# A pairwise attention kernel: exponentials for three slots at a time, the background work in one long turn per three

## The chip, the cores and the metric

The kernel runs on one core of one Trainium2 chip. The metric is the device time of that core in microseconds, from one launch; the numbers quoted are medians over several runs.

## The reference

Eight images of 128 channels and 36 x 36 points pass through three stages. The first is a convolutional attention layer (group norm, 3 x 3 convolutions for keys, values and queries, a softmax attention, two 1 x 1 convolutions, a residual). The second takes each point as a token and computes additive attention within an image of 1296 tokens; it is where nearly all the time goes. The third is a small mixture of experts.

```
def _L1_attn_ref(x, mask, Wq, bq, Wk, bk, w, bw):
    q = jnp.einsum('bld,ed->ble', x, Wq) + bq
    k = jnp.einsum('bld,ed->ble', x, Wk) + bk
    t = jnp.tanh(q[:, :, None, :] + k[:, None, :, :])
    scores = jnp.einsum('bijd,d->bij', t, w) + bw[0]
    attn = jax.nn.softmax(scores, axis=-1)
    return jnp.einsum('bij,bjd->bid', attn, x)
```

The tanh stands between every query and every key, so there are 1296 x 1296 scores of 128 terms each for every image.

## The kernel before, in words

The tanh of a sum of a query's and a key's value is written as a quotient. Five or six feature channels are taken together: with products of exponentials over all sign patterns, a matrix product over 32 or 64 rows gives a common denominator d, and another, with weighted queries, the numerator n. The score is the sum of n/d over 24 such groups. The quotient is n * exp(-ln d).

**Units and slots.** A unit is one image b, one chunk c of 432 queries (three per image) and one tile j of keys: ten tiles of 128 keys and one remainder tile of 16, which stands sixth in the order (line 919). A full unit has 12 slots (lines 49 to 54), in the repeating order five, five, six: a slot with fives has two products over 32 rows each, a slot with sixes two over 64 rows each. The halves of the array that the fives use alternate, so the numerators of slot p and the denominators of slot p + 3 fit beside each other. Every product is a 432 column float32 matmul into one PSUM bank, and each is two matmul instructions in the profile. A remainder unit has two slots. In all there are 240 full units and 24 remainders, 2928 slots. I call three slots in sequence a three; a full unit has four.

**A slot's work** (lines 1113 to 1146). In iteration p: `take_turns` runs background steps that are not matmuls; `numerators(p)` issues two matmuls into two banks of the pool `ps_n` (tag n, four banks in all); `denominators(p + LAG)`, with LAG 3, issues the matmuls for three slots later into a buffer of two banks of `ps_d` (two such buffers, four banks in all), and on ScalarE the logarithm of both banks at once (line 972) into a tile lq; each odd slot also issues the exponential over the tile's two slots (line 975). Then `terms(p)` multiplies n by lq on VectorE. In eight of the 12 slots it writes the products to rp (line 1003), and GpSimd adds them up (lines 1010 and 1012). In the four of `DVE_PAIRS` VectorE does both itself: two multiplies in place in PSUM (line 997, in the unit's first such slot 992 and 993) and two additions (line 999, in the first 994); those banks come free with the last addition. At a unit's end GpSimd folds the two sums (lines 1019 and 1021), and seven slots later ScalarE takes the score's exponential (line 1032).

**The background.** Everything else (layer 0 of the next image, its tokens and key features, the query features, weighing the tokens with the finished scores, the gate) is written as generators in four lanes: `first_of_all` (query blocks and remainders), `urgent` (the attending), `gates` and `background` (line 1067). A generator yields ahead of a matmul step or of another step, with a number of slots to rest. A matmul step takes a bank of the same pool `ps_n` through `aux`, and a later step empties it, on VectorE or ScalarE. `matmul_turn` (line 1077) runs after each slot and issues at most one matmul step: matmuls are counted in columns in `behind`, and `balance` gets PACE columns per slot; lanes other than `first_of_all` wait when the balance is negative or the next slot is one of `DVE_PAIRS`. The step that empties the bank follows in `take_turns` of the next slot (TAKE has a rest of 1), and not in a slot of `DVE_PAIRS`. Key tiles are written to DRAM and come back through SyncE's queue two units ahead (`prefetch`).

Each engine runs its instructions in the order of the program text; a pool's buffers are handed out in turn, and a new use waits for the last reader of the old one.

Of the kernel before, what the change touches and what calls it, by code (L numbers as in the profile page):

```python
# [10 lines left out]
F32 = mybir.dt.float32  # L11
# [9 lines left out]
CH = 432  # L21
# [6 lines left out]
NKT = len(KT)  # L28
# [17 lines left out]
NF = 8  # L46
FIVES = 4 * 5 * (NF // 2)

SLOTS = []
# [6 lines left out]
IN_TURN = [m + i for m in range(NF // 2) for i in (0, NF // 2)]  # L56
LAG = 3
SHIFT = 6.5
DVE_PAIRS = (2, 5, 8, 11)
PACE = 400  # L60

# [7 lines left out]
def kernel(  # L71
# [58 lines left out]
    with ExitStack() as loop, ExitStack() as score:  # L130

        def pool(name, bufs, stack=loop, side="left", space=bass.MemoryType.SB):
            return stack.enter_context(
                tc.tile_pool(name=name, bufs=bufs, side=side, space=space)
            )
# [7 lines left out]
        kfp = pool("kfp", 3, score, "right")  # L143
        kstp = pool("kstp", 3, score, "right")
        qfp = pool("qfp", NF + 1, score, "right")
        lp = pool("lp", 3, score, "right")
        rpp = pool("rpp", 3, score, "right")
        acc = pool("acc", 2, score, "right")
        ps_d = pool("ps_d", 2, score, "right", bass.MemoryType.PSUM)
# [119 lines left out]

        TAKE = (False, 1)

        def step(rest=1):
            return (False, rest)
# [645 lines left out]
        slots = []  # L921
        for u, (b, c, j) in enumerate(units):
            slots += [(u, k) for k in range(len(REM_SLOTS) if j == NKT - 1 else NP)]
        kf_of, qf_of, lq_of, live = {}, {}, {}, {}

        def prefetch(u):
            if u < len(units) and u not in kf_of:
# [9 lines left out]
        def new_block(b, c, q):  # L937
            qf = qfp.tile([128, 2, CH], F32, tag="qf", name="qf")
            qf_of[b, c, q] = qf
            return query_block(b, c, q, qf)  # L940
# [13 lines left out]
                    mm(out[32 * i : 32 * i + 32, :CH], kf[rows, q, :32],  # L954
                       qf_of[b, c, q][rows, part, :], start=True, stop=True)

        def banks(u, k):
            return 2 if units[u][2] < NKT - 1 else len(REM_SLOTS[k])

        def denominators(p):  # L960

            if p >= len(slots):
                return
            u, k = slots[p]
            d = ps_d.tile([128, 2, 512], F32, tag="d", name="d")
            n = banks(u, k)
            products(u, k, 0, [d[:, h, :] for h in range(n)])
            if k % 2 == 0:
                lq_of[u, k // 2] = lp.tile([128, 4, CH], F32, tag="lq", name="lq")
            lq = lq_of[u, k // 2]  # L970
            o = 2 * (k % 2)
            nc.scalar.activation(lq[:, o : o + n, :], d[:, :n, :CH], AF.Ln)  # L972
            if k % 2 == 1:
                some = lq[:, : o + n, :]
                nc.scalar.activation(some, some, AF.Exp, scale=-1.0)  # L975

        def numerators(p):
            ns = [ps_n.tile([128, 512], F32, tag="n", name="n") for _ in range(banks(*slots[p]))]
            products(*slots[p], 1, ns)
            return [ps[:, :CH] for ps in ns]  # L980

        def terms(p, ns):

            u, k = slots[p]
            lq = lq_of[u, k // 2]
            o = 2 * (k % 2)
            mult = nc.vector.tensor_mul
            rem = units[u][2] == NKT - 1
            if k in DVE_PAIRS and not rem:
                if k == DVE_PAIRS[0]:  # L990
                    live["d"] = acc.tile([128, CH], F32, tag="accd", name="accd")
                    mult(live["d"], ns[0], lq[:, o, :])
                    mult(ns[1], ns[1], lq[:, o + 1, :])
                    nc.vector.tensor_add(live["d"], ns[1], live["d"])
                else:
                    for h in range(2):
                        mult(ns[h], ns[h], lq[:, o + h, :])  # L997
                    for h in range(2):
                        nc.vector.tensor_add(live["d"], ns[h], live["d"])  # L999
            else:  # L1000
                rp = rpp.tile([128, 2, CH], F32, tag="rp", name="rp")
                for h, n in enumerate(ns):
                    mult(rp[:, h, :], n, lq[:, o + h, :])  # L1003
                if rem:
                    live.setdefault("rem", []).extend(rp[:, h, :] for h in range(len(ns)))
                elif k == 0:
                    live["r"] = rp
                elif k == 1:
                    live["p"] = acc.tile([128, 2, CH], F32, tag="accp", name="accp")
                    nc.gpsimd.tensor_add(live["p"], live["r"], rp)  # L1010
                else:
                    nc.gpsimd.tensor_add(live["p"], live["p"], rp)  # L1012
            if k % 2 == 1:
                lq_of.pop((u, k // 2))

        def sums(u):

# [56 lines left out]
                if lane.due(p, False) and (k not in DVE_PAIRS or lane is first_of_all):  # L1074
                    lane.run(p)

        def matmul_turn(p, k):


            before = behind[0]  # L1080
            for lane in lanes:
                while lane.due(p, True) and behind[0] == before:
                    paced = balance[0] < 0 or k + 1 in DVE_PAIRS
                    if lane is not first_of_all and paced or lane is gates and urgent:
                        break
                    lane.run(p)
            balance[0] = min(balance[0] - (behind[0] - before) + PACE, 2 * PACE)

        drain(normal(0))
        for name in ("wv_t", "wq_t"):  # L1090
# [9 lines left out]
        a_q, a_k, cs_s, fb_s, eb_s = (feat[n] for n in ("a_q", "a_k", "cs_s", "fb_s", "eb_s"))  # L1100
        drain(tokens(0), keys(0, order[:1]))
        for i, q in enumerate(IN_TURN):
            if i < 3:
                drain(new_block(0, 0, q))
            else:
                first_of_all.append(new_block(0, 0, q))
# [6 lines left out]
        for p, (u, k) in enumerate(slots):  # L1113
            b, c, j = units[u]
            rem = j == NKT - 1
            if k == 0:
                prefetch(u + 2)
                if c == 0 and j == 1:
                    if b > 0:
                        gates.append(gating(b - 1))  # L1120
                    if b == NB - 1:
                        gates.append(residuals(4))
                    if b + 1 < NB:
                        background.extend(
                            (normal(b + 1), conv_keys(b + 1), layer0(b + 1), tokens(b + 1),
                             keys(b + 1, range(NKT)))
                        )
            take_turns(p, k)
            ns = numerators(p)
            denominators(p + LAG)  # L1130
            terms(p, ns)
            if pending and pending[0][0] <= p:
                exps(p, *pending.popleft()[1:])
            last = p + 1 == len(slots) or slots[p + 1][0] != u

            if j == order[-1] and u + 1 < len(units) and k % 3:
                used = IN_TURN.index(SLOTS[k][0]) + 1
                if used < NF:
                    first_of_all.append(new_block(*units[u + 1][:2], IN_TURN[used]))
            elif j == order[-2] and last and u + 2 < len(units):  # L1140
                first_of_all.append(new_block(*units[u + 2][:2], IN_TURN[0]))
            matmul_turn(p, k)
            if last and rem:
                first_of_all.append(rem_scores(p, u, live.pop("rem")))
            elif last:
                pending.append((p + 7, u, sums(u)))
# [211 lines left out]
```

The softmax here doesn't subtract the row's maximum and nothing guards it: scores larger than these inputs give would overflow.

## Time and profile before

| | |
|---|---|
| median of 3 runs | 6133.27 us (6131.81 to 6136.31) |
| the profiled execution: span | 6139.0 us, all of its own time |
| mean granted TensorE clock | 0.985 |
| ScalarE, Ln over 864 (line 972) | 2928 times, mean 878 ns |
| ScalarE, Exp over 1728 (line 975) | 1440 times, mean 1644 ns; 24 over 1296, 1284 ns |
| VectorE multiply to rp (line 1003) | 3912 times, mean 600 ns |
| VectorE's own multiplies and sums (lines 997, 999) | 1440 times each, mean 608 and 602 ns |
| GpSimd add over 864 (line 1012) | 1440 times, mean 2025 ns |

The slot loop runs from about 162 us to 5984 us of the span; what lies before is the first image's setup, what comes after is the experts. In the lines that follow, a group is given by its line, its engine and its operation, then the tile written and the tiles read, the shape and the count. In a timeline a line starts with the start and the duration in us, and a bracket at the end tells how long the engine was idle and what ended that. A wait is given as who waited, for whom, the sum in us, the number of waits and the longest. PE is TensorE, PEld its weight loads, DVE VectorE, ACT ScalarE, POOL GpSimd, SP SyncE.

### The profile page before, as it was taken

How to read it: one execution, taken by the hardware profiler on the slowest of the kernel's cores; microseconds unless marked ns; L12 is line 12 of the kernel's file. 1: busy time of each engine (PE TensorE's matmuls, PEld its weight loads, DVE VectorE, ACT ScalarE, POOL GpSimd, SP SyncE). 2: the span in 40 equal slices, each digit the busy share in tenths (PEclk: the TensorE clock that was granted, in tenths of full speed). 3: DMA queues.
4: the chain of work that ended last, by engine and by line, in shares of the span. 5: the costliest groups of instructions: out<-in, count | busy, mean ns of one | idle time of the engine just before them, and what ended most of it. 6: DMA issues, size and time to landing. Idle time of an engine off the chain costs nothing.

```text
span 6139.0 us, 93072 instructions
## 1 busy us (share of the span) xinstructions
PE 5957.9 (97%) x33480; PEld 2862.1 (47%) x33480; DVE 4796.4 (78%) x9521; ACT 5279.9 (86%) x5371; POOL 4597.7 (75%) x2819
## 2 busy tenths in 40 slices
PE   7999999999999999999999999999999999999996
PEld 5454444544544445444455444454444544544443
DVE  4787878877788787877888777887778877788882
ACT  1888898888988888889998889888898888999990
POOL 4777777777787777778778786877777777787870
PEclk9999999999999999999999999999999999999997
DMA  1210011100110002100111001110011100110008
GB/s 44 70 37 22 25 62 38 34 25 28 68 43 20 26 27 71 39 24 23 44 55 39 22 24 59 44 39 22 20 65 40 34 25 28 58 50 29 28 20 297
DMA packets 151519, 270.87 MB, mean 44 GB/s; under 512 B 45648, under 2 KB 76752, under 8 KB 151056
## 3 DMA queue, kind: packets, MB, share of 16 engines
q1 hardware_dynamic: 151056, 264.92, 13.0%
q8 instruction: 264, 4.33, 0.3%
q14 instruction: 199, 1.63, 0.1%
HBM read 200.41 MB, written 64.19 MB: 43 GB/s over the span
## 4 chain that ended last, share of the span: by engine, by line
PE 77%; ACT 7%; DVE 6%; issue 6%; POOL 2%; DMA 1%; SPq 0%; DVEq 0%; POOLq 0%; ACTq 0%
PE n L949 37%; PE d L949 12%; PE pa L284 7%; PE pc L284 5%; ACT lq L972 5%; PE s L284 3%; PE pk L284 3%; PE pq L284 3%; DVE rp L1003 2%; DVE n L997 1%; DVE accd L999 1%; PE d L954 1%; ACT lq L975 1%; DMA w<-in_weight_dram 1%; PE n L954 1%
## 5 line engine op out<-in xcount | busy, mean ns | idle before, releaser
L1012 POOL TENSOR_TENSOR accp<-accp,rp 128x864 f32<-128x864 f32 x1440 | 2915.8, 2025 | 1041.0 <-DVE rp L1003 948.8
L949 PE MATMUL n<-qf,kf 32*128 32x432 f32 (+1 forms) x11520 | 3325.3, 574 | 46.5 <-ACT e L1032 13.3
L949 PE MATMUL d<-qf,kf 32*128 32x432 f32 (+1 forms) x11520 | 2991.6, 561 | 38.7 <-ACT lq L972 38.2
L972 ACT ACTIVATE lq<-d 128x864 f32<-128x864 f32 x2928 | 2524.2, 878 | 542.6 <-PE d L949 512.1
L1003 DVE TENSOR_TENSOR rp<-n,lq 128x432 f32<-128x432 f32 x3912 | 2173.3, 600 | 743.5 <-PE d L949 542.8
L975 ACT ACTIVATE lq<-lq 128x1728 f32<-128x1728 f32 (+1 forms) x1464 | 2398.2, 1638 | 46.3
L949 PEld LDWEIGHTS n<-qf,kf 32*128 32x128 f32 (+1 forms) x11520 | 1206.4, 184 | 1600.3 <-DVE rp L1003 581.5
L949 PEld LDWEIGHTS d<-qf,kf 32*128 32x128 f32 (+1 forms) x11520 | 1090.0, 185 | 422.1 <-issue 224.7
L997 DVE TENSOR_TENSOR n<-n,lq 128x432 f32<-128x432 f32 x1440 | 814.9, 608 | 142.1 <-PE n L949 88.5
L999 DVE TENSOR_TENSOR accd<-n,accd 128x432 f32<-128x432 f32 x1440 | 866.3, 602 | 24.6
L1010 POOL TENSOR_TENSOR accp<-rp 128x864 f32<-128x864 f32 x240 | 485.2, 2022 | 197.7 <-DVE rp L1003 195.6
L711 POOL TENSOR_SCALAR qf<-qf,cs_s 128x432 f32<-128x432 f32 x192 | 260.9, 1365 | 45.0 <-ACT qf L710 44.4
L284 PEld LDWEIGHTS pa<-xh,e 128*108 128x108 f32 x1920 | 222.5, 174 | 131.1 <-DVE rp L1003 56.0
L1021 POOL TENSOR_TENSOR accd<-accp,accd 128x432 f32<-128x432 f32 x240 | 265.2, 1105 | 18.8
L1019 POOL TENSOR_TENSOR accp<-accp 128x432 f32<-128x432 f32 x240 | 264.4, 1102 | 16.7
L284 PE MATMUL pa<-xh,e 128*108 128x129 f32 x1920 | 262.9, 283 | 8.7 <-ACT e L1032 5.2
L284 PE MATMUL s<-q,k 128*116 128x432 f32 x480 | 230.3, 568 | 1.7 <-DVE q L316 1.4
L284 PEld LDWEIGHTS pk<-xT,a_k 128*128 128x128 f32 x1408 | 171.2, 192 | 107.0 <-DVE n L997 33.7
L462 POOL TENSOR_TENSOR tot<-tot,e 116x432 f32<-116x432 f32 x192 | 212.0, 1104 | 6.0 <-ACT e L471 4.6
L471 ACT ACTIVATE e<-s 116x432 f32<-116x432 f32 x240 | 124.9, 520 | 98.3 <-PE s L284 97.9
L284 PE MATMUL pa<-e,vw 116*128 116x432 f32 x480 | 204.6, 549 | 0.0
L284 PE MATMUL pk<-xT,a_k 128*128 128x128 f32 (+1 forms) x1408 | 202.5, 287 | 0.1
(213 smaller groups left out, 3788.4 us busy)
## 6 DMA issues: line engine op xcount, KB each, us to landing
kf<-kd SPq DMA_DIRECT2D x239, 512.0 KB
kd<-ks SPq DMA_DIRECT2D x158, 256.0 KB
w<-in_weight_dram SPq DMA_DIRECT2D x32, 1024.0 KB
wk_t<-wk_t_d SPq DMA_DIRECT2D x7, 768.0 KB
wv_t<-wv_t_d SPq DMA_DIRECT2D x7, 768.0 KB
wq_t<-wq_t_d SPq DMA_DIRECT2D x7, 768.0 KB
x<-in_x_dram SPq DMA_DIRECT2D x8, 648.0 KB
t<-tokd SPq DMA_DIRECT2D x96, 54.0 KB
```

The costliest lines, as they stand in the source:

```text
L284: mm(out, lhsT, rhs, **kw)
L711: nc.gpsimd.tensor_scalar(qf[:, 1, :], qf[:, 0, :], cs_s[:, q : q + 1], None, ALU.mult)
L949: mm(outs[h][:, :CH], kf[rows[h], q, :], qf_of[b, c, q][rows[h], part, :], start=True, stop=True)
L972: nc.scalar.activation(lq[:, o : o + n, :], d[:, :n, :CH], AF.Ln)
L975: nc.scalar.activation(some, some, AF.Exp, scale=-1.0)
L997: mult(ns[h], ns[h], lq[:, o + h, :])
L999: nc.vector.tensor_add(live["d"], ns[h], live["d"])
L1003: mult(rp[:, h, :], n, lq[:, o + h, :])
L1010: nc.gpsimd.tensor_add(live["p"], live["r"], rp)
L1012: nc.gpsimd.tensor_add(live["p"], live["p"], rp)
L1019: nc.gpsimd.tensor_add(s[:, 0, :], s[:, 0, :], s[:, 1, :])
L1021: nc.gpsimd.tensor_add(d, s[:, 0, :], d)
```

## The change

The parts, in order of the diff:

- VectorE's own sums move from the third slot of each three to the first, and the background gets its matmul turn only in that first slot (`TURNS`), with a credit of 380 columns per slot, up to 1520. A turn goes on until the credit is below zero or no lane has a matmul step due, and after each matmul step the steps that are due, such as emptying the bank, are issued at once (TAKE's rest is 0).
- The query blocks of the next unit follow a table (`NEXT_AT`), two after each of three slots; the last of them is made in the next chunk's first unit. One more is made ahead of the loop.
- Denominators come ahead of numerators in an iteration, except where the lq buffer is released by the same slot's multiplies (`late`).
- A tile lq holds six banks, for three slots; there are two of them instead of three of four banks. Groups end with the first slot of a three, or with the first of a remainder, so a group is the second and third slot of one three and the first of the next.
- GpSimd's first sum takes slots 1 and 2 instead of 0 and 1.

```diff
-DVE_PAIRS = (2, 5, 8, 11)
-PACE = 400
+DVE_PAIRS = (0, 3, 6, 9)
+TURNS = (0, 3, 6, 9)
+NEXT_AT = {3: IN_TURN[1:3], 6: IN_TURN[3:5], 9: IN_TURN[5:7]}
+PACE = 380
...
-        lp = pool("lp", 3, score, "right")
+        lp = pool("lp", 2, score, "right")
...
-        TAKE = (False, 1)
+        TAKE = (False, 0)
...
+        group_of, ends, at = {}, [-1], 0
+        for p, (u, k) in enumerate(slots):
+            group_of[p] = (len(ends), at)
+            at += banks(u, k)
+            rem = units[u][2] == NKT - 1
+            if p + 1 == len(slots) or (k == 0 if rem else k % 3 == 0):
+                assert at <= 6
+                ends.append(p)
+                at = 0
...
-            if k % 2 == 0:
-                lq_of[u, k // 2] = lp.tile([128, 4, CH], F32, tag="lq", name="lq")
-            lq = lq_of[u, k // 2]
-            o = 2 * (k % 2)
+            g, o = group_of[p]
+            if o == 0:
+                lq_of[g] = lp.tile([128, 6, CH], F32, tag="lq", name="lq")
+            lq = lq_of[g]
             nc.scalar.activation(lq[:, o : o + n, :], d[:, :n, :CH], AF.Ln)
-            if k % 2 == 1:
+            if p == ends[g]:
                 some = lq[:, : o + n, :]
                 nc.scalar.activation(some, some, AF.Exp, scale=-1.0)
...
-                elif k == 0:
+                elif k == 1:
                     live["r"] = rp
-                elif k == 1:
+                elif k == 2:
...
-        def matmul_turn(p, k):
-
-
-            before = behind[0]
-            for lane in lanes:
-                while lane.due(p, True) and behind[0] == before:
-                    paced = balance[0] < 0 or k + 1 in DVE_PAIRS
+        def matmul_turn(p, turn):
+
+
+            balance[0] = min(balance[0] + PACE, 4 * PACE)
+            while True:
+                for lane in lanes:
+                    paced = not turn or balance[0] < 0
                     if lane is not first_of_all and paced or lane is gates and urgent:
+                        continue
+                    if lane.due(p, True):
                         break
+                else:
+                    return
+                before = behind[0]
+                lane.run(p)
+                balance[0] -= behind[0] - before
+                while lane.due(p, False):
                     lane.run(p)
-            balance[0] = min(balance[0] - (behind[0] - before) + PACE, 2 * PACE)
...
-            if i < 3:
+            if i < 4:
...
-            ns = numerators(p)
-            denominators(p + LAG)
-            terms(p, ns)
+            ahead = p + LAG
+            g, o = group_of.get(ahead, (0, 1))
+            late = o == 0 and g > 2 and ends[g - 2] == p
+            if not late:
+                denominators(ahead)
+            terms(p, numerators(p))
+            if late:
+                denominators(ahead)
...
-            if j == order[-1] and u + 1 < len(units) and k % 3:
-                used = IN_TURN.index(SLOTS[k][0]) + 1
-                if used < NF:
-                    first_of_all.append(new_block(*units[u + 1][:2], IN_TURN[used]))
+            if j == order[-1] and u + 1 < len(units):
+                for q in NEXT_AT.get(k, ()):
+                    first_of_all.append(new_block(*units[u + 1][:2], q))
+            elif j == order[0] and k == TURNS[0] and u > 0:
+                first_of_all.append(new_block(b, c, IN_TURN[-1]))
...
-            matmul_turn(p, k)
+            matmul_turn(p, k == 1 if rem else k in TURNS)
```

More of the change, by code (lines that the diff above doesn't have):

```diff
@@ L923, with banks @@
             slots += [(u, k) for k in range(len(REM_SLOTS) if j == NKT - 1 else NP)]
+        def banks(u, k):
+            return 2 if units[u][2] < NKT - 1 else len(REM_SLOTS[k])
         kf_of, qf_of, lq_of, live = {}, {}, {}, {}
+        group_of, ends, at = {}, [-1], 0
[7 more added lines that the diff above has]
+                at = 0
         def prefetch(u):
@@ L955, in products @@
                        qf_of[b, c, q][rows, part, :], start=True, stop=True)
-        def banks(u, k):
-            return 2 if units[u][2] < NKT - 1 else len(REM_SLOTS[k])
         def denominators(p):
@@ L984, in terms @@
             u, k = slots[p]
-            lq = lq_of[u, k // 2]
-            o = 2 * (k % 2)
+            g, o = group_of[p]
+            lq = lq_of[g]
             mult = nc.vector.tensor_mul
@@ L1012, in terms @@
                     nc.gpsimd.tensor_add(live["p"], live["p"], rp)
-            if k % 2 == 1:
-                lq_of.pop((u, k // 2))
+            if p == ends[g]:
+                lq_of.pop(g)
         def sums(u):
```

## The prediction, before the result was known

> **What bounds the kernel now.** I read first the page's busy shares and its chain that ended last, then stretches of the loop, then single instructions, then the waits.
>
> ```profile
> PE 5957.9 (97%) x33480; PEld 2862.1 (47%) x33480; DVE 4796.4 (78%) x9521; ACT 5279.9 (86%) x5371; POOL 4597.7 (75%) x2819
> ...
> PE 77%; ACT 7%; DVE 6%; issue 6%; POOL 2%; DMA 1%; SPq 0%; DVEq 0%; POOLq 0%; ACTq 0%
> ```
>
> TensorE carries most of the chain, but its busy time contains waits, so stages must be told apart. I took the start of each unit (12 slots, or 4 threes) from its first numerator matmul. The stretches below, from the view of engine sums by stretch, are one unit each: without background, with layer 0's scores, and with keys.
>
> ```profile
> 5685.95:5705.85 19.90, 19.24 (x99) 7.68 (x97) 16.67 (x32) 19.71 (x20) 16.79 (x10) 1.00 0.09 29
> ...
> 2033.17:2058.00 24.83, 24.83 (x117) 9.11 (x117) 17.81 (x33) 22.71 (x25) 20.07 (x14) 1.00 0.06 18
> 2303.39:2328.67 25.28, 25.28 (x162) 14.40 (x161) 17.48 (x32) 24.70 (x29) 17.46 (x10) 1.00 0.29 102
> ```
>
> After length come PE, PEld, DVE, ACT, POOL. Without background ScalarE is full (19.71 of 19.90): **4.98 us per three**. With background TensorE is, and a unit takes 21 to 27 us. Over the full units of the first seven batches (210, ten to a chunk) I find a mean of 24.1 us, **6.04 us per three**; 18 units of the last batch, at under 21.6 us, have next to no background.
>
> Single instructions, from the timeline without background:
>
> ```profile
> 5688.97 1.65 ACT L975 ACTIVATE lq<-lq 128x1728 f32<-128x1728 f32 x1
> ...
> 5690.52 1.65 ACT L972 ACTIVATE lq<-d 128x864 f32<-128x864 f32 x2
> ...
> 5692.20 1.64 ACT L975 ACTIVATE lq<-lq 128x1728 f32<-128x1728 f32 x1
> ```
>
> An Exp of 1728 holds ScalarE 1.55 us until the next Ln; two Ln and the step to their Exp take 1.68 (0.77 between Ln starts, 0.92 from an Ln's start to the Exp that reads it). 6 x 3.23 plus 0.55 for the score's exp (line 1032) makes the unit. With background:
>
> ```profile
> 2039.33 0.63 PE L949 MATMUL n<-qf,kf 32*128 32x432 f32 x2
> ...
> 2040.27 1.72 PE L284 MATMUL pa<-e,vw 116*128 116x432 f32 x4
> ...
> 2041.93 0.63 PE L949 MATMUL d<-qf,kf 32*128 32x432 f32 x2
> ...
> 2042.85 1.00 PE L949 MATMUL n<-qf,kf 64*128 64x432 f32 x4
> 2043.04 1.12 DVE L1003 TENSOR_TENSOR rp<-n,lq 128x432 f32<-128x432 f32 x2 [0.41 <-PE d L949]
> 2043.04 0.89 ACT L972 ACTIVATE lq<-d 128x864 f32<-128x864 f32 x1 [0.75 <-PE d L949]
> ...
> 2044.08 1.12 DVE L997 TENSOR_TENSOR n<-n,lq 128x432 f32<-128x432 f32 x2
> ...
> 2044.50 0.98 PE L284 MATMUL s<-q,k 128*116 128x432 f32 x2
> 2045.11 1.24 DVE L999 TENSOR_TENSOR accd<-n,accd 128x432 f32<-128x432 f32 x2
> ```
>
> From start to start: a five's n and d together 0.94 (2039.33 to 2040.27), two background matmuls 1.65, a six's n and d in sequence 1.65 (2042.85 to 2044.50), one background matmul 0.92. So a matmul streams 0.72, and 0.2 comes on top where the kind changes. Ln starts 1.1 after its d. VectorE's own sums take 2.27: the first bank is free 1.65 after their start, the second at the end. What TensorE waits for:
>
> ```profile
> PEld n L949 <- DVE rp L1003: 581.5, 1032, 1.5
> ...
> PEld n L949 <- DVE accd L999: 198.5, 472, 1.6
> ...
> PEld d L949 <- ACT lq L972: 146.1, 199, 5.0
> ```
>
> Part of the first is the 0.62 that a weight load idles while a matmul streams, but it also says that the numerator banks, handed back by VectorE, hold TensorE, more than the denominator banks do.
>
> **The skill.** "TensorEngine Tiling (Array Packing)", Key Properties, says that changing the tiling mode drains TensorE; the 0.2 us above agrees. "ScalarE: Activation LUTs", What ACT_TABLE_LOAD costs, gives 186 ns plus 0.833 ns per element, and 93 ns of overlap; this trace has 1644 for 1728 elements and 1284 for 1296 (0.833 each, 204 over), and starts 94 ns before the previous end. "TensorE: Matmul & The Clock Gate", Step-by-step, says that only weight loads are pulled ahead while matmuls stay in program order; the timeline agrees, so one waiting numerator holds all that is behind it.
>
> **The change part by part.** A, B, C are the three slots.
>
> *Exp for three.* Exps fall from 1464 to about 985. One of 2592 holds ScalarE 1.55 + 0.72 (two more banks at 0.36) = 2.27. Per three 1.5 x 1.55 becomes 2.27, and the step into an Exp (0.92 against 0.77) comes once instead of 1.5 times: 4.86 becomes 2 x 0.77 + 0.92 + 2.27 = 4.73, a gain of 0.13. But there are still two denominator buffers. While an Exp runs TensorE can prepare two denominators; the third needs the first Ln done: 0.87 + 0.05 + 1.1 = 2.02 until its Ln, where 1.54 was wanted. ScalarE's cycle becomes 2.02 + 0.92 + 2.27 = 5.21, with the score's exp **5.35 against 4.98**. Bounds: the shortest d-to-Ln in the trace is about 1.0 (5.25); background evictions that fell into the gap would hide it, but they stand behind the Exp.
>
> *One long background turn at A.* Two turns per three become one: up to one drain, 0.2, saved. But its tiles come from the same four numerator banks. Allocation is A, A, m background tiles, B, B, C, C. With m = 2, B's banks are A's own, and A is now what VectorE sums itself. The loop, from the start of C's denominators: numerators start 0.83 later and end at 1.71; C's multiplies 1.78 to 2.82; own sums to 5.1; B's second numerator 5.12, and 0.93 later the next C: **6.07**. With m = 1 the last bank needed is A's first: 4.5, so **5.45**. With m = 3 a background tile itself must be emptied: behind the own sums (about 6.8) or, on ScalarE, behind an Exp of 2.36 (7.35): **about 7.1**. In the first three of a unit (own sums of three operations) about 5.35, 5.35, 5.85 and 6.8 for m = 0 to 3. TensorE itself asks less: 1.65 + 2 x 0.93 + background of about 1.7 = 5.2.
>
> How many tiles: per batch 36 convolution, 30 score and 15 value tiles, 22 of keys, 24 of queries, 24 of attending, about 50 others: 201 over 120 threes, 1.68. With shares of 0.05, 0.35, 0.45, 0.15 for m = 0 to 3 (my choice; steps are 300 to 900 columns against 1140 of credit) the mean is 5.97, with unit firsts **5.93**. An even split of 1 and 2 gives 5.83, the low end. Nothing incidental is in that. The same reasoning for the kernel before (own sums at C, one tile in each of two turns) gives 0.94 to the end of C's numerators plus 1.65 + 0.93 + 0.9 + 0.93, some 5.65 with the wait for B's multiplies, and it takes 6.04: 0.39 of incidental waits. Steps and evictions in one place should avoid more than half of these; I add 0.15 (0 to 0.39): **6.08**.
>
> *Denominators first.* Ln gets its input sooner; a six's numerators start 0.72 later, which is in the loop above. For fives nothing: n and d run beside each other. If d waits, n, the turn and everything behind wait; ScalarE has over 0.5 to spare in the 6.07 loop.
>
> *VectorE's sums moved to A; TAKE 0.* Same instruction counts. Evictions follow the sums at once, up to 1.3 us, within the 0.9 to 1 that VectorE has free before B's multiplies (Exp's end) in most threes; where it isn't, as in attending, up to 0.5, inside the added 0.15. GpSimd's adds start a slot later, same count: 4.2 of 6 us. Query blocks: same matmuls, exps and GpSimd products, one moved out of the last unit (26.3 us, GpSimd-bound: 17 + 7 x 1.33): 0. DMAs issued by moved steps go through SP, whose engines are 6 to 29% busy in those stretches: 0; if that cover failed, a late key tile would stop TensorE. lq keeps its 5184 columns. One query block more before the loop: 1 to 2 us.
>
> *Remainder.* Its groups are irregular, and a late denominator waits for the multiplies: I take +0.5 us, 24 times (-0.5 to +1.5): +12.
>
> **The sum**, against the profiled execution (span 6139.0, which leaves nothing outside it; the runs' median is 5.7 lower): 840 threes x 0.04 = +34; 72 threes of the last batch x 0.37 = +27; remainder +12: +73, less the 5.7: **6206 us**.
>
> **Rivals.** *Faster: the drains and stalls go.* Place: the 840 threes with background; price: 5.83 instead of 6.04, -176, with +27 left in the last batch and -12 at remainders: about 5975; half of the -176 gives about 6060. It decides once the mean three falls under about 6.0. For it: TensorE's own need falls to 5.2. Against it: the numerator loop doesn't go through TensorE's rate. *Clearly slower: the ring of banks.* If m = 3 is common and incidental waits stay at 0.39: 6.32 per three, +235 + 27 + 36: about 6430; half of that excess gives about 6280. For it: evictions by ScalarE stand behind a longer Exp. *Nothing seen*: both cancel, 6133. That the change fails to do what it says isn't possible for the group sizes; the long turn could stay short if lanes are seldom ready, which gives 5.35 to 5.45 in light threes and heavier ones elsewhere, near the forecast.
>
> **Chances.** Forecast (6145 to 6280) 0.45; clearly slower 0.14; nothing 0.08; faster 0.33. A measurement here tells about 0.2% from no change, so faster 0.33, same 0.08, slower 0.59. Own range of the forecast: 6145 to 6280. The range 6010 to 6340 leaves out about one in ten on each side.
>
> **What would show it.** Right: Ln waiting for PE d about 0.4 to 0.5 once per three in stretches without background, a unit there near 21.4 us; B's numerators waiting for line 999's operation; units of 23 to 25 us with background; Exp of 2592 at about 2.36. Wrong: background units at 23 or less, no wait at B, or a third Ln that follows at 0.77.

## The result, and the profile after

The changed kernel takes 6459.85 us (median of 4 runs, 6445.48 to 6470.23) against 6134.65 us: the ratio is 1.0529, with a 95% interval of 1.0513 to 1.0544. It is slower by 5.3%, where 1.2% was forecast; the time lies above the stated range. The profiled execution has a span of 6468.5 us, 329.5 more than before, and 326.3 of these lie in the slot loop (6130.3 against 5804.0 from the first slot to the start of the last unit).

The page's shares and chain, answering to those shown of the kernel before:

```profile
PE 6020.5 (93%) x33480; PEld 2924.7 (45%) x33480; DVE 4789.2 (74%) x9521; ACT 5241.5 (81%) x4892; POOL 4603.8 (71%) x2819
...
PE 69%; ACT 15%; issue 10%; DVE 4%; POOL 1%; DMA 1%; SPq 0%; DVEq 0%; POOLq 0%; ACTq 0%
```

ScalarE has 479 instructions fewer and 38 us less to do, as was meant. But the chain that ended last has moved: TensorE's share is 8 points lower, ScalarE's 8 higher, and that of issue 4 higher. The other engines have the same number of instructions. TensorE's busy time, which contains waits, is 62.6 us longer; the engines wait for each other.

One more thing differs. TensorE's granted clock falls to half for stretches of 3.4 to 10.2 us. In the slot loop before there are 16 of them, 88.7 us in all, and now 44, 252.6 us (mean clock over the loop 0.992 before, 0.979 after). One of them in the view by stretch, where the number after the five engines is the clock, with a six's denominators and numerators from the timeline:

```profile
1779.02:1785.82 6.80, 6.80 (x25) 2.95 (x24) 3.79 (x11) 2.86 (x4) 2.00 (x1) 0.50 0.09 33
...
1781.65 1.81 PE L964 MATMUL d<-qf,kf 64*128 64x432 f32 x4
...
1783.25 1.65 PE L964 MATMUL n<-qf,kf 64*128 64x432 f32 x4
...
1784.83 1.09 PE L964 MATMUL d<-qf,kf 32*128 32x432 f32 x2
```

The two take 3.18 us here, from 1781.65 to 1784.83, and 1.65 us at full clock (1905.92 to 1907.57). An estimate: if matmuls take twice as long, a stretch costs at most half its length, so the clock accounts for at most 82 us of the 326 (half of 252.6 less half of 88.7). No run holds the clock, so how much it costs isn't shown, nor why it falls.

A unit (12 slots) of each of three kinds from the view of sums by stretch; after the length come the busy times of PE, PEld, DVE, ACT and POOL, then the clock. The first two are the same units as before, without background and with layer 0's scores; the third is the unit that held keys before, and here holds few:

```profile
5990.89:6012.07 21.18, 17.68 (x99) 8.90 (x99) 16.79 (x32) 19.80 (x18) 16.33 (x9) 1.00 0.08 25
2131.44:2156.69 25.25, 24.61 (x126) 11.52 (x125) 20.27 (x38) 21.52 (x21) 18.35 (x12) 1.00 0.06 21
2423.42:2445.60 22.18, 20.07 (x124) 9.60 (x123) 16.67 (x31) 20.37 (x21) 17.49 (x13) 1.00 0.18 55
```

Without background a unit takes 21.18 instead of 19.90 us, and ScalarE is no longer full. The instructions of that stretch, in the timeline, show why:

```profile
5995.11 1.65 ACT L984 ACTIVATE lq<-d 128x864 f32<-128x864 f32 x2
...
5996.04 0.63 PE L964 MATMUL d<-qf,kf 32*128 32x432 f32 x2 [1.03 <-ACT lq L984]
...
5997.08 0.89 ACT L984 ACTIVATE lq<-d 128x864 f32<-128x864 f32 x1 [0.31 <-PE n L964]
...
5998.00 2.36 ACT L987 ACTIVATE lq<-lq 128x2592 f32<-128x2592 f32 x1
...
6000.27 1.65 ACT L984 ACTIVATE lq<-d 128x864 f32<-128x864 f32 x2
6000.45 1.12 DVE L1015 TENSOR_TENSOR rp<-n,lq 128x432 f32<-128x432 f32 x2 [0.82 <-ACT lq L987]
```

The first line is two logarithms, for slots B and C of a three. The third one's denominators can start at 5996.04, when the first logarithm (0.87) is over and its buffer free; their logarithm follows 1.04 later, the exponential 0.92 after that, and the next logarithm 2.27 after that: 0.93 + 1.04 + 0.92 + 2.27 = 5.16 us, from 5995.11 to 6000.27. It is a loop through ScalarE and TensorE: three of the unit's four threes take just these 5.16 us, and the fourth, with the score's exponential, 5.70. (ScalarE's wait is put down to the numerators because they were issued beside the denominators.) VectorE's multiplies start only after the whole exponential.

The waits, after those of before that answer to them and weren't shown yet (the three that were are 581.5, 198.5 and 146.1 us):

```profile
L972 ACT ACTIVATE lq<-d 128x864 f32<-128x864 f32 x2928 | 2524.2, 878 | 542.6 <-PE d L949 512.1
DVE rp L1003 <- ACT lq L975: 49.0, 55, 4.0
```

```profile
L984 ACT ACTIVATE lq<-d 128x864 f32<-128x864 f32 x2928 | 2517.0, 883 | 887.0 <-PE n L964 647.5
PEld d L964 <- ACT lq L984: 939.9, 1190, 4.4
ACT lq L984 <- PE n L964: 647.5, 987, 4.6
...
DVE rp L1015 <- ACT lq L987: 432.4, 428, 4.6
PEld n L964 <- DVE accd L1011: 217.4, 574, 1.2
...
PEld n L964 <- DVE rp L1015: 80.9, 209, 1.6
```

TensorE now waits for the denominator buffers (939.9 us, 146.1 before), ScalarE sits idle ahead of its logarithms for 887.0 us (542.6 before), and VectorE waits for the exponential (432.4, 49.0 before). The numerator banks hold TensorE little more than before at the sums (217.4 against 198.5), and much less at the other multiplies (80.9 against 581.5). Part of TensorE's two large figures comes from the order alone, as the instruction that stands first takes the wait: with pairs and the same order (e1, below) 879.1 of the 939.9 us are still there. What pairs take away is ScalarE's idle time (604.0) and VectorE's wait for the exponential (none is listed).

With a long turn of three tiles, in the first three of the unit that starts at 1900.16 us:

```profile
1900.14 0.63 PE L964 MATMUL d<-qf,kf 32*128 32x432 f32 x2 [0.64 <-ACT lq L984]
...
1901.50 3.55 PE L286 MATMUL pc<-xwin,wv_t 128*128 128x216 f32 x18
...
1902.11 2.37 ACT L987 ACTIVATE lq<-lq 128x2592 f32<-128x2592 f32 x1
...
1904.98 0.63 PE L964 MATMUL d<-qf,kf 32*128 32x432 f32 x2
...
1906.02 1.83 ACT L984 ACTIVATE lq<-d 128x864 f32<-128x864 f32 x2 [1.55 <-PE n L964]
...
1907.57 0.63 PE L964 MATMUL d<-qf,kf 32*128 32x432 f32 x2
```

Here it is the other way round. TensorE works on the background from 1901.50 to 1904.98, the exponential ends at 1904.48, and ScalarE has nothing to do for 1.55 us, since the next denominators stand behind the turn. From one first slot's denominators to the next this three takes 7.43 us.

By the number of background tiles (the PSUM banks that a three's background matmuls fill, counted from the starts of the numerators in the trace), threes of batches 1 to 6 (the first being 0) take, as mean us with their number; e1 and e8, below, have the numbers of the changed kernel:

| tiles | before | after | pairs (e1) | split (e8) |
|---|---|---|---|---|
| 0 | 4.51 (79) | 5.45 (114) | 5.06 | 5.03 |
| 1 | 5.47 (144) | 5.66 (210) | 5.45 | 5.54 |
| 2 | 6.37 (443) | 6.51 (288) | 6.39 | 6.76 |
| 3 | 6.90 (54) | 7.72 (84) | 7.55 | 7.35 |
| 4 and more | none | 8.51 (24) | 8.65 | 8.58 |

Before, 111 of 720 threes took under 4.9 us: after a heavy three came a light one in which TensorE caught up (the three ahead of a light one took 6.60 us on average, that ahead of any other 5.92). In the changed kernel only 6 do; in e1 90 do, in e8 95. The long turns make threes more unequal, and with the loop of 5.16 us there are next to no light ones to even them out.

### The profile page after: what moved, and what is told of

Read it like the earlier page. It is cut to its first block, busy times and chain, and to the rows that moved or that the text cites. A ratio compares the mean times of both kernels' runs of the same rounds, so it can differ in the third digit from the quotient of the medians.

```text
span 6468.5 us, 91491 instructions
## 1 busy us (share of the span) xinstructions
PE 6020.5 (93%) x33480; PEld 2924.7 (45%) x33480; DVE 4789.2 (74%) x9521; ACT 5241.5 (81%) x4892; POOL 4603.8 (71%) x2819
## 4 chain that ended last, share of the span: by engine, by line
PE 69%; ACT 15%; issue 10%; DVE 4%; POOL 1%; DMA 1%; SPq 0%; DVEq 0%; POOLq 0%; ACTq 0%
PE d L964 29%; PE n L964 18%; ACT lq L984 8%; PE pa L286 6%; PE pc L286 4%; ACT lq L987 4%; PE s L286 3%; PE pk L286 2%; PE pq L286 2%; DVE rp L1015 1%; ACT e L1044 1%; DVE n L1009 1%; PE n L969 1%; PE d L969 1%; DMA w<-in_weight_dram 1%
## 5 line engine op out<-in xcount | busy, mean ns | idle before, releaser
L964 PE MATMUL n<-qf,kf 32*128 32x432 f32 (+1 forms) x11520 | 3384.7, 572 | 36.2 <-DVE rp L1015 16.9
L984 ACT ACTIVATE lq<-d 128x864 f32<-128x864 f32 x2928 | 2517.0, 883 | 887.0 <-PE n L964 647.5
L964 PE MATMUL d<-qf,kf 32*128 32x432 f32 (+1 forms) x11520 | 2911.4, 581 | 198.1 <-ACT lq L984 194.2
L987 ACT ACTIVATE lq<-lq 128x2592 f32<-128x2592 f32 (+2 forms) x985 | 2300.8, 2336 | 31.2
L964 PEld LDWEIGHTS d<-qf,kf 32*128 32x128 f32 (+1 forms) x11520 | 923.8, 187 | 1720.1 <-ACT lq L984 939.9
L964 PEld LDWEIGHTS n<-qf,kf 32*128 32x128 f32 (+1 forms) x11520 | 1335.6, 188 | 735.5 <-DVE accd L1011 217.4
L286 PE MATMUL s<-q,k 128*116 128x432 f32 x480 | 209.3, 548 | 3.8 <-DVE accd L1011 1.7
L1004 DVE TENSOR_TENSOR accd<-n,lq 128x432 f32<-128x432 f32 x240 | 144.1, 601 | 66.9 <-PE n L964 63.8
```

Of the source, the lines that this page charges most:

```text
L286: mm(out, lhsT, rhs, **kw)
L964: mm(outs[h][:, :CH], kf[rows[h], q, :], qf_of[b, c, q][rows[h], part, :], start=True, stop=True)
```

## The experiments

All figures are medians; the ratio is to the kernel before, run on the same chip, with its 95% interval.

**Undo the group of three** (e1): pairs again for lq (three buffers of four banks) and the exponential, all else as changed; the late denominators, which only groups of three need, go too.

```diff
...
-            g, o = group_of[p]
+            g, o = (u, k // 2), 2 * (k % 2)
             if o == 0:
-                lq_of[g] = lp.tile([128, 6, CH], F32, tag="lq", name="lq")
+                lq_of[g] = lp.tile([128, 4, CH], F32, tag="lq", name="lq")
...
-            if p == ends[g]:
+            if k % 2 == 1:
...
```

> The changed kernel with the exponential back over two slots (lq of four banks, three of them); the long turn, VectorE's sums in the first slot and denominators first stay. If the two denominator buffers are what costs (the third Ln of a group waits for a denominator that waits for the first Ln), nearly all comes back: about 6150 to 6200 us, and units without background fall from 21.2 to 19.9 us. If the ring of four numerator banks under the long turn is what costs, only the light threes gain: 6370 to 6410 us, with threes of three or more background tiles still at 7.4 us and more.

Measured 6247.22 us, 1.0187 (1.0157 to 1.0217): 213 of the 325 us come back. The unit without background is back at 19.95 us, with the least busy TensorE of all:

```profile
5781.71:5801.66 19.95, 14.49 (x100) 5.55 (x99) 16.79 (x31) 19.76 (x20) 16.33 (x10) 1.00 0.08 26
```

The order of all other instructions is the same, so threes can be compared one by one over the whole loop: those without background tiles lose 0.36 us each to the group of three, with one tile 0.23, with two 0.14, with three 0.17. 138 of the 201 us in these sums are in threes with no tile or one. The group of three costs most where there is least to do, which is the denominator buffers' mark. The clock isn't what it costs: e1 has 238.9 us at half clock in the loop, nearly as many. Of the two readings the first is nearer, though not all came back.

**The group of three alone, in the kernel before** (e2), with two lq buffers, and denominators after the multiplies where a remainder's group needs it.

```diff
...
-            if k % 2 == 0:
-                lq_of[u, k // 2] = lp.tile([128, 4, CH], F32, tag="lq", name="lq")
-            lq = lq_of[u, k // 2]
-            o = 2 * (k % 2)
+            g, o = group_of[p]
+            if o == 0:
+                lq_of[g] = lp.tile([128, 6, CH], F32, tag="lq", name="lq")
+            lq = lq_of[g]
...
-            if k % 2 == 1:
+            if p == ends[g]:
...
```

> The kernel before with one part alone: the exponential over three slots (and a late denominator after the multiplies where a remainder's group needs it). Denominator buffers: units without background 21.2 us, and most of the loss is here, 6350 us or more. Ring of banks under the long turn: only units that ScalarE bounds lose, 6150 to 6220 us.

Measured 7360.95 us, 1.2003 (1.1918 to 1.2088). That lies in the first reading's open range, but far beyond what it had in mind: a unit without background takes 24.8 us (that of 19.90 before), not 21.2. Its waits:

```profile
ACT lq L982 <- PE d L962: 1652.2, 1353, 3.5
DVE rp L1013 <- ACT lq L985: 1413.5, 718, 5.7
PEld n L962 <- DVE rp L1013: 921.9, 1235, 2.5
```

With numerators first the loop is longer: the multiplies wait for the exponential (1413.5 us), numerators wait for banks that those multiplies hold (921.9), and the denominators of the next group's last slot stand behind these numerators, so that ScalarE waits for them (1652.2). Denominators first is what makes groups of three bearable.

**VectorE's sums back in the third slot** (e3), and **the turns of before** (e4: at most one matmul step after a slot, emptied in the next, 400 columns).

```diff
-DVE_PAIRS = (0, 3, 6, 9)
+DVE_PAIRS = (2, 5, 8, 11)
...
```

> The changed kernel with VectorE's own sums back in the third slot of a three (2, 5, 8, 11); the long turn stays in the first. Ring of banks: the banks of the first slot's numerators come back after one multiply each, so threes with two background tiles fall from about 6.2 to 5.5 or 5.7 us; 6200 to 6300 us in all. Denominator buffers: no change, 6430 to 6470 us.

```diff
-PACE = 380
+PACE = 400
...
-        TAKE = (False, 0)
+        TAKE = (False, 1)
...
-            matmul_turn(p, k == 1 if rem else k in TURNS)
+            matmul_turn(p, k)
```

> The changed kernel with the turns of before (at most one matmul step after a slot, the bank emptied in the next slot, 400 columns of credit); exponentials of three, sums in the first slot and denominators first stay. Ring under the long turn: threes with three and more tiles in a row are gone, 6200 to 6280 us. Denominator buffers: 6430 us or more.

Measured 6567.08 us, 1.0709 (1.0678 to 1.0740), and 6577.94 us, 1.0726 (1.0695 to 1.0757): each is over 100 us worse than the changed kernel. The reading by the ring of numerator banks, on which most of the forecast's working rested, expected 6200 to 6300 and 6200 to 6280, and falls as the main cause. The reading by the denominator buffers allowed e4 (6430 or more), but not e3, which it expected at 6430 to 6470. With two tiles and the sums moved away a three takes 6.69 us, not less than 6.51.

**Denominators first alone** (e5), in the kernel before.

```diff
-            ns = numerators(p)
-            denominators(p + LAG)
-            terms(p, ns)
+            denominators(p + LAG)
+            terms(p, numerators(p))
```

> The kernel before with one part alone: the denominators ahead of the numerators. If the order costs, because a six's numerators start 0.72 us later and a denominator that waits holds the numerators behind it, 1 to 2% more: 6200 to 6250 us. If the group of three and the turns make up the whole loss, 6110 to 6150 us.

Measured 6293.97 us, 1.0250 (1.0233 to 1.0267): this order costs by itself, as the first reading had it, and more than its 6200 to 6250. TensorE's wait for the denominator buffers' logarithm rises from 146.1 us:

```profile
PEld d L949 <- ACT lq L972: 457.7, 656, 4.9
```

VectorE's own multiplies, which are the sixes', wait 428.9 us for numerators (88.5 before). Numerators held behind a denominator that waits, and a six's that start later in any case, both fit this; the run doesn't tell them apart. The clock has little to do with it (95.6 us at half clock in the loop).

**Pairs with the turns of before** (e6: e1 and the edit of e4) and **pairs with the sums in the third slot** (e7: e1 and the edit of e3).

> The changed kernel with pairs for the exponential and the turns of before; VectorE's sums in the first slot and denominators first stay. If the long turn is what the pairs left of the loss (6247 against 6133), because threes with three or more tiles take over 7 us, 6130 to 6170 us. If the sums in the first slot are, 6230 us or more; and since short turns cost 118 us with groups of three, it may be worse than 6247.

> The changed kernel with pairs for the exponential and VectorE's sums back in the third slot; the long turn and denominators first stay. If the banks that the sums hold are the rest of the loss, 6140 to 6180 us. If the long turn is, 6240 us or more. With groups of three the sums in the third slot cost 107 us more, so with pairs the same may show: 6300 us.

Measured 6459.67 us, 1.0524 (1.0503 to 1.0545), and 6392.93 us, 1.0415 (1.0394 to 1.0436). Neither undone part gives anything back; the two last sentences of the expectations, that it may get worse, are what came.

**Two exponentials to a group** (e8): groups of three kept, one exponential over the first two slots after their logarithms, one over the third after its own.

```diff
-            if p == ends[g]:
-                some = lq[:, : o + n, :]
+            if p == ends[g] or o == 2:
+                some = lq[:, 4 if o == 4 else 0 : o + n, :]
```

> The changed kernel with groups of three kept, but two exponentials to a group: one over the first two slots after their Ln, one over the third after its own. More instructions, yet the third denominator is made beside the first exponential. If the cost of the group is the third Ln's wait (Ln, then denominator, then Ln), the floor of a three falls from 5.16 us to about 5.0 and light threes catch up again: a unit without background 20.3 to 20.7 us, 6250 to 6330 us in all. If the cost is that an exponential of the group ends late for the multiplies, little changes: 6420 to 6480 us.

Measured 6409.51 us, 1.0442 (1.0421 to 1.0463). The timeline without background shows the third slot's denominators (5952.30) made beside the second logarithm. The first exponential now runs while the logarithm that reads them would have waited, and there is no wait ahead of that logarithm at 5954.61:

```profile
5952.30 0.63 PE L964 MATMUL d<-qf,kf 32*128 32x432 f32 x2 [0.56 <-ACT lq L984]
...
5953.06 1.64 ACT L987 ACTIVATE lq<-lq 128x1728 f32<-128x1728 f32 x1
...
5954.61 0.87 ACT L984 ACTIVATE lq<-d 128x864 f32<-128x864 f32 x1
5955.51 0.93 ACT L987 ACTIVATE lq<-lq 128x864 f32<-128x864 f32 x1
...
5956.34 0.87 ACT L984 ACTIVATE lq<-d 128x864 f32<-128x864 f32 x1
```

Such units take 19.7 to 20.4 us. Compared one by one with the changed kernel, threes without tiles gain 0.36 us and with one tile 0.17, about what pairs gave them. For units without background that shows the third logarithm's wait as the cause, since the loop of 5.16 us makes up their whole time. For light threes among background it isn't shown alone: the split also lets the multiplies of two slots start earlier, and VectorE's wait for the exponential falls from 432.4 to 13.1 us. But threes with two tiles lose 0.24, those whose tiles ScalarE empties most (scores 0.46, keys 0.34, queries 0.38 us): ScalarE has 148 us more to do (5389.9 against 5241.5). So the gain is 50 us only. The total lies between the two readings, 10 us from the second, for which the exponential's late end is the cost, and 80 from the first. By the totals e8 doesn't decide; by the units without background (20.3 to 20.7 expected) it speaks for the first.

**Pairs with numerators first** (e9: e1 with the order of before), **the long turn alone** (e10: that, with the sums in the third slot too, so the kernel before with the long turn and the query blocks' table), and **the changed kernel with numerators first** (e11).

```diff
-            terms(p, numerators(p))
+            ns = numerators(p)
...
+            terms(p, ns)
```

> The changed kernel with pairs for the exponential and the numerators first again; the long turn and VectorE's sums in the first slot stay. If denominators first costs with pairs what it cost alone (about 155 us) and the parts add up, 6247 - 155: 6080 to 6110 us, faster than before. If a long turn behind a late denominator makes up for it, 6240 us or more.

> The kernel before with the long turn (in the first slot of a three, 380 columns, banks emptied at once) and the query blocks' table alone: pairs, numerators first, VectorE's sums in the third slot. If the parts add up, 6393 - 155: 6220 to 6260 us. If the uneven load of long turns is a loss only because threes cannot catch up, close to before: 6120 to 6180 us.

> The changed kernel with the numerators first again, nothing else. If groups of three need the denominators first, because numerators wait for banks whose multiplies wait for the group's exponential, and the next group's last denominator is queued behind them, it nears the 7361 us of the groups alone: 6900 to 7300 us. If the order is a small matter, 6400 to 6500 us.

Measured: e9 6370.86 us, 1.0385 (1.0367 to 1.0402); e10 6298.52 us, 1.0264 (1.0244 to 1.0285); e11 6805.47 us, 1.1090 (1.1068 to 1.1113). e9 is a miss of its first case and falls in its second, which was open upwards: costs don't add up, and with the long turn and early sums denominators first is worth 124 us where it cost 156 alone. e10 lies somewhat above its first case. e11 lies just below its first case and confirms e2: groups of three need the denominators first.

**The sums in the first slot alone** (e12), in the kernel before.

```diff
-DVE_PAIRS = (2, 5, 8, 11)
+DVE_PAIRS = (0, 3, 6, 9)
...
-                elif k == 0:
+                elif k == 1:
                     live["r"] = rp
-                elif k == 1:
+                elif k == 2:
```

> The kernel before with VectorE's own sums in the first slot of a three alone (the turns' rule moves with them: no paced turn in the slot ahead of the sums). If the place of the sums costs by itself, as it did with denominators first and short turns (6294 to 6460 us), 6270 to 6320 us. If it matters only with denominators first, 6120 to 6160 us.

Measured 6488.27 us, 1.0573 (1.0543 to 1.0604): the place costs by itself, by more than was expected (6270 to 6320).

**What is left with pairs.** Three more runs asked where e1's 113 us come from: e1 with numerators first for the sixes only (e13), e1 with at most three tiles to a turn (e14), and the changed kernel with numerators first for the sixes only (e15).

```diff
+            ns = numerators(p) if k % 3 == 2 else None
...
-            terms(p, numerators(p))
+            terms(p, ns or numerators(p))
```

```diff
+            tiles = 0
...
-                    paced = not turn or balance[0] < 0
+                    paced = not turn or balance[0] < 0 or tiles >= 3
...
+                tiles += behind[0] > before
```

> The changed kernel with pairs for the exponential, and the numerators first in the third slot of a three (the sixes) alone; the fives keep denominators first. If the 113 us that the pairs left come from the sixes' numerators starting 0.72 us late, which delays VectorE's sums and the banks they hold, 6140 to 6190 us. If they come from the long turns themselves, 6230 to 6270 us.

> The changed kernel with pairs for the exponential and at most three background tiles in a long turn (query blocks not counted out). If the 113 us come from the longest turns (threes with four tiles and more take 8.6 us), 6170 to 6220 us. If they come from the threes with one and two tiles, 6235 to 6260 us.

> The changed kernel, groups of three kept, with the numerators first in the third slot alone. If the sixes' late numerators are a part of the loss by themselves, 6360 to 6410 us. If with groups of three the third Ln's denominator, which then follows 0.72 us later, matters more, 6500 us or more.

Measured: e13 6453.20 us, 1.0516 (1.0486 to 1.0547); e14 6229.88 us, 1.0152 (1.0123 to 1.0182); e15 6744.19 us, 1.0990 (1.0958 to 1.1022). The sixes' late numerators aren't the loss: bringing them forward costs 206 us with pairs, outside what e13's two cases allowed, and 284 us with threes, as e15's second case had it. The tail of long turns is worth about 17 us, if anything: e14 lies between its two cases, its ratio's interval overlaps that of e1, and it has 164 us at half clock where e1 has 239. Of e1's 104 us in the loop 32 are in the remainders, where more background now runs. The half clock can account for up to 75 of the 104, by the same estimate as above (238.9 us against 88.7). It isn't denominators first that brings it: alone, the long turn has 208 us of it (e10), the early sums 218 (e12), denominators first 96 (e5).

All measured combinations of these four parts, in us:

| order | turns | sums in | pairs | threes |
|---|---|---|---|---|
| numerators first | short | third slot | 6135 (before) | 7361 |
| denominators first | short | third slot | 6294 | not tried |
| numerators first | short | first slot | 6488 | not tried |
| denominators first | short | first slot | 6460 | 6578 |
| numerators first | long | third slot | 6299 | not tried |
| numerators first | long | first slot | 6371 | 6805 |
| denominators first | long | third slot | 6393 | 6567 |
| denominators first | long | first slot | 6247 | 6460 (after) |

No version beat the kernel before. In every row that has both, groups of three cost: 118 to 1226 us. Every other part costs when it is alone; together they mend each other in part.

## Why the prediction was wrong, step by step

**Direction and the exponential's loop: right, the size wrong.** The forecast was 1.2% slower; 5.3% came. In number this is nearly its rival "clearly slower", priced at about 6430 us; the forecast's own range ended at 6280, half of that rival's excess. Half of this is luck: the rival named the ring of banks as the place, which the runs don't bear out, though the waits that it took over from the kernel before did come.

**Exp for three: right.** Its loop was put at 5.21 us, or 5.35 with the score's exponential: 5.16 and 5.30 came (21.18 a unit, less 4 x 5.16, leaves 0.54). The exponential of 2592 takes 2.364 us, as worked out, and the next logarithm starts 2.27 after it. e1 and e8 show it in the units without background.

**The step that failed: the incidental waits, and "ScalarE has over 0.5 to spare".** The forecast set 5.93 us per three for the ring of banks, and added 0.15 of incidental waits out of a range to 0.39. With the tile numbers that came, 0.16, 0.29, 0.40, 0.12 and 0.03 for none to four and more, its own prices still give about 5.9, so the choice of shares did no harm. But a three took 6.30 us in the first seven batches (25.20 a unit): 0.37 of waits, two and a half times the term, and nearly all that the kernel before had. 840 threes lost 222 us instead of 34. It was wrong to expect that steps in one place would avoid waits. With pairs (e1) the same threes take 6.10 us: 0.20 of the 0.37 belongs to the group of three. The reserve of 0.5 was reckoned inside one three at its mean; with a loop of 5.16 us a light three has little time to make up for a heavy one. e1 fits this: of 223 us in the loop 201 lie in the threes, compared one by one, and 138 of these in the light ones. That is the likely way, not a proven one, since VectorE's wait for the long exponential goes away with pairs too. The forecast had no term for the clock, either: of the 0.37, up to 0.14 is time at half clock, by the estimate above (229 us in the first seven batches), 0.05 of which the kernel before has too. The prices themselves fit unequally: threes with no tile took 5.45 where 5.35 was set, those with two 6.51 instead of 6.07.

**The ring of numerator banks: there, but not the main cause.** B's numerators do wait for the sums' addition (217.4 us), yet moving the sums away (e3) made the kernel slower by 107 us, and shortening the turns (e4) by 118 us. The forecast held the long turn and the early sums to be the places of the loss; given the group of three and denominators first they are gains.

**Denominators first: mis-sized.** It was put at nothing beyond the sixes' 0.72 us. Alone it costs 156 us (e5), probably because numerators that could run wait behind a denominator, and a six's start later; with groups of three its absence costs 346 us (e11).

**Remainders and the last batch.** Remainder units were to cost 0.5 us each and cost 2.57 in the first seven batches (54 us against 12), none in the last batch, where there is no background. The trace has background matmuls in all 21 remainders of the first seven batches, in 7 of them before, so part is only moved. The last batch was to cost 27 us, counted for 18 of its units, and costs 51: the other units were put at nothing, and among them are those with the gate's transposes, of which the one from 5894.12 to 5921.87 takes 27.75 instead of 20.18 us.

**What was taken from the Trainium skill.** The drain at a change of tiling mode ("TensorEngine Tiling (Array Packing)", Key Properties) was never the larger term: the forecast put up to 0.2 us per three on it. The price per element of "ScalarE: Activation LUTs", What ACT_TABLE_LOAD costs, held for the new size: 2364 ns is 0.833 per element and 205 over, where the page has 186.

**Left open.** The 113 us that remain with pairs (e1) are told apart only in part: not the sixes' order (e13), about 17 us of tail at best (e14), 32 us in the remainders, and up to 75 us at half clock, which overlap. Since parts mend each other, no sum of single costs explains them, and no run settles it. A third denominator buffer, the direct remedy for the third logarithm's wait, wasn't tried: the eight PSUM banks are all in use.

## What to carry to other kernels

When an instruction is made to cover more of a pipeline's steps, count the buffers ahead of it: with two buffers a group of two can be prepared beside the long instruction, and the third member turns into a serial loop through two engines. The group of three cost 213 of 325 us here, to save 38 us of ScalarE's time. Judge a schedule not by its mean step but by whether a light step can make up for a heavy one; a fixed loop time near the mean leaves little room for it. And price waits that aren't understood at what the kernel before shows of them, not at less.

## What the runs showed of the hardware that wasn't expected

In the loop without background a logarithm starts 1.04 us after the first of its denominator matmuls, and denominators start 0.06 us after the end of the logarithm that frees their buffer; this round trip of 0.93 + 1.04 us against 0.77 us for a logarithm that follows its predecessor is the price of the third buffer that isn't there. And the same order of two matmul groups, denominators ahead of numerators, cost 156 us in one schedule and saved 346 us in another; such an edit can't be judged alone. The granted clock fell to half in 16 stretches of the loop before and in 44 after, and a six's two products then took 3.18 instead of 1.65 us; the stretches are other ones under another schedule, so the clock is worth reading beside the waits.
